# Conv block on one core: input loads ahead of the branch, tables inside the timetable, early and late steps on other engines, and a GELU output sorted by phase

## The chip, the core and the metric

The kernel runs on one core of a Trainium2 chip. A core has TensorE (PE, matrix products), VectorE (DVE), ScalarE (ACT, activation functions), GpSimd (POOL) and SyncE (SP, which here only issues transfers), and 16 DMA engines that move data between HBM and the on-chip memory SBUF. Products land in PSUM, which has eight banks. Each engine works through its own instruction list in order and waits on semaphores for the others. The metric is the device time of one execution, in microseconds (us), lower is better.

## The reference

The input x has 16 samples of 256 channels on a 64 x 64 grid, in fp32. Two residual layers follow one another. Cut to what matters:

```
x = x + L0(gn(x))      # gn: group norm, 32 groups of 8 channels
x = x + L1(gn(x))

L0: xn = rmsnorm over channels
    q, k, v = w_qkv @ xn             # 4 heads of 32
    q = softmax over head channels;  k = softmax over pixels
    context = k v^T;  out = context^T q * scale
    out = rmsnorm(w_out @ out + b_out)

L1: router: softmax of a 256 -> 4 product of the pooled input, the best 2 experts, renormalised
    expert: depthwise 3x3 conv + bias, gelu, 256 x 256 pointwise product + bias
    out = weighted sum of the two chosen experts
```

## The kernel before

A small head loads the attention weights w_qkv, multiplies them by the norm's weights and tests on DVE whether all logits are small. All engines read that flag and branch: here into `pipelined_path`; the other branch, `general_path`, is not executed.

**Order of the work.** The pipelined path writes its order out by hand. Each step is a small function with a key. A table PLAN gives each key a place in "slots"; the place of a step is the start of its phase for its sample, plus its group's offset, plus PLAN[key]. All steps are sorted by place and issued in that order, so PLAN fixes every engine's instruction list. A sample's period is 64 slots. Five phases run staggered, so that several samples are under way at once: "in" (first statistics of sample b), "q" (projections and attention context, 8 groups of 512 pixels), "out" (attention output, again 8 groups), "route" (second statistics, router, choice of experts), and "x" (the experts, 4 quarters of 16 rows). Sample 0 has nothing before it, sample 15 nothing behind it.

**The steps by line.** The rows of x that end up as output live in a ring of seven tiles; L117 loads them, for sample 0 right after the branch. For the statistics of later samples L244 loads a second copy (xa) and L247 a third (xb) for the norm, each in pieces of 512 KB (both halves of the channels), two buffers each. Statistics are L253 on DVE; L263 and L274 are small PE products of the group norm. The norm is L293 on ACT. PE transposes (L301), ACT squares and sums per token (L308), the scale r is made by L228 on DVE and L229 (a power) on POOL. With r ACT writes the scaled transposed pixels (L314, `x_keep`) and, after the projection on PE (L330), the exponentials (L338). PE adds up the context (L348); DVE and POOL normalise q (L358, L359, L363), PE turns it (L371), ACT keeps it (L374). L381 to L416 mix the context with w_out; L413 is that product, called pm. In "out" PE forms po (L424), ACT its squares (L432), DVE the scaled output ob (L443, `out_norm`), PE turns it back (L450), DVE adds it to the ring (L459), ACT squares it for the second norm (L466). The router's product pz is L509.

In "x" the experts work on two halves of the channels. The first half goes through PE: ACT pads it (L641), SP writes it to HBM and reads it back spread over partitions (`lay`, `spread`, tiles xr, 12 buffers), PE multiplies it by taps (L701), ACT applies GELU (L709). The second half goes through DVE: ACT pads it (L683) and starts the accumulator acc (L716), DVE adds eight taps for each of the two experts (L723, a 128 x 1024 operation), ACT applies GELU in place (L730). The pointwise product adds both halves up in four PSUM banks, one for each phase q (row and column odd or even): L742 multiplies acc, reading every second column of every second row, and L750 multiplies xr with 32-row tiles. DVE adds the result and the bias to the ring (L759, `residual`), SP stores it (L765). The blended expert weights come from L573 and L575 on DVE.

**Constants.** The weights for all this are loaded on ACT's queue at the start of the branch (L169 to L197), 25 transfers, and 36 small DVE operations (L209) build a table of taps from them.

Of the kernel before, what the change touches and what calls it, by code (L numbers as in the profile page):

```python
# [46 lines left out]
FC = 4 * (QA + 1) * PC  # L47
NRING = 7
# [4 lines left out]
    "load_a": -9.25, "stats": -5.66, "load_b": -8.65, "load_x1": -2.78, "mean": 2.06, "means": 2.28,  # L53
    "dev": 3.53, "devs": 8.08, "scale": 11.68, "bias": 12.33, "in_lead": 22.04, "norm0": -5.62,
    "norm1": -0.47, "turn_x0": 0.51, "x_sq0": 1.33, "x_sq1": 1.55, "turn_x1": 1.24, "x_sq2": 2.35,
    "x_sq3": 2.12, "token": 3.32, "x_keep0": 5.33, "x_keep1": 5.35, "x_keep2": 4.92,
    "x_keep3": 4.95, "project0": 4.29, "evacuate0": 5.68, "project1": 5.03, "evacuate1": 5.72,
    "project2": 5.43, "evacuate2": 6.67, "project3": 5.62, "evacuate3": 6.89, "context": 8.15,
    "q_sum": 8.09, "q_norm": 14.32, "q_turn": 15.88, "q_keep": 16.2, "mix_a": 9.74,
    "mix_turn": 9.95, "mix_v": 10.71, "mix_vv": 11.24, "mix_b": 12.36, "mix_out": 13.21,  # L60
    "mix_c": 13.7, "mix_lead": 15.67, "attend0": -0.09, "out_sq0": 0.05, "out_sq1": 0.62,
    "out_scale0": 1.38, "out_norm0": 2.98, "attend1": 0.36, "out_sq2": 1.1, "out_sq3": 1.41,
    "out_scale1": 2.74, "out_norm1": 3.53, "out_turn0": 4.46, "out_add0": 5.46, "sq_sums0": 6.37,
    "out_turn1": 5.51, "out_add1": 6.2, "sq_sums1": 7.31, "sums1": 7.7, "means1": 7.87,
    "scale1": 8.76, "router": 9.2, "route": 10.86, "choose": 12.26, "pick_taps": 15.66,
    "route_lead": 22.33, "pick_rows0": 12.84, "pick_rows1": 18.67, "pick_row_bias": 15.38,
    "weigh": 19.46, "pick_bias": 20.95, "pick000": 0.61, "pick100": 10.24, "pick001": 0.9,
    "pick101": 13.08, "pick002": 6.46, "pick102": 13.36, "pick003": 8.1, "pick103": 14.74,
    "pick010": 1.08, "pick110": 14.45, "pick011": 2.05, "pick111": 15.05, "pick012": 2.43,
    "pick112": 15.56, "pick013": 5.56, "pick113": 16.03, "lay_pw": 11.73, "spread_pw": 12.85,  # L70
    "taps0": 7.52, "taps1": 10.69, "taps2": 0.05, "taps3": -1, "taps4": 8.36, "taps5": -2.07,
    "taps6": 1.95, "taps7": 12.86, "pad1": -8.93, "start0": -2.18, "tap01": 0.61, "tap02": 0.96,
    "tap03": 1.88, "tap04": 2.18, "tap05": 2.73, "tap06": 3.26, "tap07": 5.03, "tap08": 5.6,
    "gelu10": 10.66, "start1": 4.35, "tap11": 6.15, "tap12": 6.65, "tap13": 9.14, "tap14": 9.65,
    "tap15": 11.78, "tap16": 12.21, "tap17": 13.12, "tap18": 14.18, "gelu11": 15.25, "pad00": 1.65,
    "pad01": 1.66, "lay": 4.1, "spread0": 6.9, "conv0": 10.23, "gelu00": 11.75, "spread1": 7.8,
    "conv1": 10.77, "gelu01": 12.39, "spread2": 5.25, "conv2": 10.75, "gelu02": 10.92,
    "spread3": 7.7, "conv3": 11.85, "gelu03": 12.31, "spread4": 8.85, "conv4": 12.79,
    "gelu04": 13.99, "spread5": 9.05, "conv5": 12.88, "gelu05": 14.21, "spread6": 8.74,
    "conv6": 12.33, "gelu06": 14.39, "spread7": 9.48, "conv7": 13.66, "gelu07": 14.86,  # L80
    "pw00": 16.34, "pw01": 17.04, "pw02": 18.31, "pw03": 18.34, "pw10": 19.06, "pw11": 21.05,
    "pw12": 21.16, "pw13": 21.82, "residual00": 20.82, "residual01": 23.29, "residual02": 24.4,
    "residual03": 25.27, "store0": 28.88, "residual10": 23.06, "residual11": 23.4,
    "residual12": 26.78, "residual13": 27.98, "store1": 29.6, "in_first": 5.27, "in_more": 21.33,
    "q_first": 9.02, "out_first": 11.84, "out_more": 4.06, "q_less": 0.28,
# [4 lines left out]
def pipelined_path(ctx, tc, wqkv, x, w_outT, b_out, g_out, router_wT, router_b, dw, dw_b, pwT, pw_b, out):  # L90
# [12 lines left out]
    ring = [const.tile([P, KH, 2, GT], FP, name=f"ring_{i}") for i in range(NRING)]  # L103
# [14 lines left out]

    for g in range(NG):
        load_x1(0, g)  # L120
# [48 lines left out]
    nc.scalar.dma_start(out=wout, in_=w_outT)  # L169

    bout = const.tile([P, C], FP, name="bout")
    nc.scalar.dma_start(out=bout, in_=b_out.to_broadcast([P, C]))
    nc.vector.tensor_scalar(bout, bout, 1.0 / NH, None, ALU.mult)
    gout = const.tile([P, KH], FP, name="gout")
    nc.scalar.dma_start(out=gout, in_=g_out.rearrange("(k p) -> p k", p=P))
    rw = const.tile([P, KH, NE], FP, name="rw")
    nc.scalar.dma_start(out=rw, in_=router_wT.rearrange("(k p) e -> p k e", p=P))
    nc.vector.tensor_scalar(rw, rw, 1.0 / TEMP, None, ALU.mult)
    rb = const.tile([P, NE], FP, name="rb")
    nc.scalar.dma_start(out=rb, in_=router_b.to_broadcast([P, NE]))  # L180
    nc.vector.tensor_scalar(rb, rb, 1.0 / TEMP, None, ALU.mult)
    dww = const.tile([P, NE, 10], FP, name="dww")
    nc.scalar.dma_start(out=dww[:, :, 0:9], in_=dw[P:C])
    nc.scalar.dma_start(out=dww[:, :, 9:10], in_=dw_b[P:C])
    pw = const.tile([P, KH, NE, C], FP, name="pw")
    nc.scalar.dma_start(out=pw, in_=pwT.rearrange("(k p) e o -> p k e o", p=P))
    pwb = const.tile([P, KH, NE], FP, name="pwb")
    nc.scalar.dma_start(out=pwb, in_=pw_b.rearrange("(k p) e -> p k e", p=P))

    dwc = const.tile([P, CGR, NE, 9], FP, name="dwc")
    btab = const.tile([P, CGR, NE], FP, name="btab")
    for v in range(NPC):
        vs = slice(v * CH, (v + 1) * CH)
        nc.scalar.dma_start(out=dwc[vs], in_=dw[0:P].rearrange("(g c) e t -> c g e t", c=CH))
        nc.scalar.dma_start(  # L197
            out=btab[vs], in_=dw_b[0:P].rearrange("(g c) e u -> c g (e u)", c=CH)
        )
    tab = const.tile([P, CGR, 2, 2, 2, NE], FP, name="tab")  # L200
    nc.gpsimd.memset(tab, 0.0)
    for o in range(2):
        for d in range(2):
            for p in range(2):
                for v in range(NPC):
                    ky, kx = v // 2 - o, 2 * d + 1 - v % 2 - p
                    if 0 <= ky <= 2 and 0 <= kx <= 2:
                        dst = tab[:, :, d, o, p]
                        nc.vector.scalar_tensor_tensor(  # L209
                            dst, dwc[:, :, :, 3 * ky + kx], piece[:, v : v + 1], dst,  # L210
                            ALU.mult, ALU.add,
                        )
# [30 lines left out]
    def load_a(b, g):  # L243
        nc.sync.dma_start(out=new(work, [P, KH, GT], "xa", b, g), in_=cols(x, b, g))  # L244

    def load_b(b, g):
        nc.sync.dma_start(out=new(work, [P, KH, GT], "xb", b, g), in_=cols(x, b, g))  # L247

    def stats(b, g):
        st = live["st", b] if g else new(small, [P, KH, NG, 6], "st", b, bufs=2)  # L250
        xa = live.pop(("xa", b, g)) if b else x1(b, g)
        for k in range(KH):
            nc.vector.bn_stats(st[:, k, g], xa[:, k])  # L253
# [34 lines left out]
    def norm(b, g, k):  # L288
        if k == 0:
            new(work, [P, KH, GT], "xg", b, g)  # L290
        xb = live["xb", b, g] if b else x1(b, g)
        bi, sc = live["bi", b][:, k : k + 1], live["sc", b][:, k : k + 1]
        nc.scalar.activation(live["xg", b, g][:, k], xb[:, k], AF.Identity, bias=bi, scale=sc)  # L293
# [18 lines left out]
    def x_keep(b, g, c):  # L312

        nc.scalar.activation(  # L314
            xt[g % 2][:, c, :C], live["px", b, g, c // 2][:, c % 2], AF.Copy,
            scale=live["r", b, g][:, c : c + 1],
        )
# [122 lines left out]
    def out_norm(b, g, hf):  # L440
        ob = new(work, [P, 2, C], "ob", b, g, hf, bufs=3)
        s = live.pop(("s", b, g, hf))
        nc.vector.tensor_tensor(  # L443
            ob, live.pop(("po", b, g, hf)), s.unsqueeze(2).to_broadcast([P, 2, C]), ALU.mult
        )
# [267 lines left out]
    def start1(b, j, i):  # L713
        ds = live["ds", b]
        acc = new(work, [P, QR, W], "acc", b, j, i, bufs=3)
        nc.scalar.activation(  # L716
            acc, pd1[j % 2][:, 0:QR, 0:W], AF.Identity,
            bias=ds[:, i, 9:10], scale=ds[:, i, 0:1],
        )
# [713 lines left out]
def block_kernel(ctx, tc, x, g_norm, w_qkvT, *weights_and_out):  # L1433
# [24 lines left out]
    with tc.If(small_logits > 0) as branch:  # L1458
        pipelined_path(tc, wqkv, x, *weights_and_out)
# [39 lines left out]
```

## Time and profile before

| | |
|---|---|
| median of 3 runs | 2748.02 us (2747.52 to 2748.82) |
| profiled execution | 2746.3 us |
| its span, first to last instruction | 2744.5 us |
| PE busy | 2634.1 us (96%), 19236 products |
| DVE busy | 2370.1 us (86%), 4384 instructions |
| ACT busy | 2127.0 us (78%), 5310 |
| POOL busy | 778.6 us (28%), 874 |
| bytes moved | 394.72 MB, 144 GB/s |
| transfers issued | 1024 of xr, 256 of ring, 120 each of xa and xb, 128 stores |

How to read it: "busy" counts the time in which an engine has an instruction in work. PE's instructions overlap, so the time from one start to the next says more of its rate than the length of one. One fp32 product is two passes over the array, and each pass is a row of the trace. A stage in which PE has gaps is set by something else, and a window of that stage shows which engine is full. The last sample's stage starts at about 2450 us, and the first product of the depthwise conv of sample 0 at 241.4 us.

### The profile page before, as it was taken

How to read it: one execution, taken by the hardware profiler on the slowest of the kernel's cores; microseconds unless marked ns; L12 is line 12 of the kernel's file. 1: busy time of each engine (PE TensorE's matmuls, PEld its weight loads, DVE VectorE, ACT ScalarE, POOL GpSimd, SP SyncE). 2: the span in 40 equal slices, each digit the busy share in tenths (PEclk: the TensorE clock that was granted, in tenths of full speed). 3: DMA queues.
4: the chain of work that ended last, by engine and by line, in shares of the span. 5: the costliest groups of instructions: out<-in, count | busy, mean ns of one | idle time of the engine just before them, and what ended most of it. 6: DMA issues, size and time to landing. Idle time of an engine off the chain costs nothing.

```text
span 2744.5 us, 54743 instructions
## 1 busy us (share of the span) xinstructions
PE 2634.1 (96%) x19236; PEld 2241.9 (82%) x19236; DVE 2370.1 (86%) x4384; ACT 2127.0 (78%) x5310; POOL 778.6 (28%) x874
## 2 busy tenths in 40 slices
PE   4988999999999999999999999999999999998978
PEld 3777888888888888888888888888888888886756
DVE  5459898998989899898988989899898988889996
ACT  3888878887887888888887887888788788875542
POOL 1233233233222322332232323323222233222110
PEclk9999999999999999999999999999999999999999
DMA  4335455464654545455454545546465444424332
GB/s 143 100 116 144 142 153 159 141 182 133 168 160 133 163 156 156 150 153 161 140 164 150 161 141 157 157 143 181 131 169 158 134 143 129 138 98 127 110 112 98
DMA packets 225867, 394.72 MB, mean 144 GB/s; under 512 B 22064, under 2 KB 104496, under 8 KB 225584
## 3 DMA queue, kind: packets, MB, share of 16 engines
q1 hardware_dynamic: 220704, 389.62, 46.7%
q8 instruction: 156, 2.56, 0.4%
q10 hardware_dynamic: 4880, 1.51, 0.3%
q14 instruction: 127, 1.04, 0.1%
HBM read 280.82 MB, written 110.23 MB: 142 GB/s over the span
## 4 chain that ended last, share of the span: by engine, by line
PE 85%; DVE 8%; ACT 3%; issue 2%; DMA 1%; POOL 1%; SPq 0%; ACTq 0%; POOLq 0%; DVEq 0%
PE pw L750 16%; PE pw L742 16%; PE pq L330 14%; PE dw L701 14%; PE po L424 7%; PE pc L348 7%; DVE acc L723 4%; PE tr L450 4%; PE px L301 4%; PE ptq L371 2%; DVE ring L759 1%; ACT junk L432 1%; ACT xt L314 1%; DVE ring L459 1%; ACT e L338 0%
## 5 line engine op out<-in xcount | busy, mean ns | idle before, releaser
L723 DVE SCALAR_TENSOR_TENSOR acc<-pd,ds,acc 128x1024 f32<-128x1024 f32 x1024 | 1314.2, 1286 | 5.7
L229 POOL TENSOR_TENSOR s<-s,mhalf 128x2 f32<-128x2 f32 x256 | 246.9, 966 | 1086.1 <-DVE s L228 958.6
L742 PE MATMUL pw<-acc,pw 128*128 128x256 f32 x2048 | 507.4, 392 | 22.7 <-ACT acc L730 12.5
L701 PE MATMUL dw<-xr,taps 128*128 128x256 f32 x2048 | 482.9, 380 | 8.7 <-ACT xr L709 6.0
L330 PE MATMUL pq<-wqkv_n,xg 128*128 128x256 f32 x2048 | 486.9, 382 | 2.9 <-DVE ring L459 2.9
L750 PE MATMUL pw<-xr,psp 32*128 32x256 f32 x8192 | 478.3, 381 | 0.0
L742 PEld LDWEIGHTS pw<-acc,pw 128*128 128x128 f32 x2048 | 377.9, 190 | 102.3 <-ACT acc L730 14.2
L750 PEld LDWEIGHTS pw<-xr,psp 32*128 32x128 f32 x8192 | 407.3, 185 | 63.4 <-issue 43.4
L701 PEld LDWEIGHTS dw<-xr,taps 128*128 128x128 f32 x2048 | 375.6, 190 | 59.6 <-ACT xr L709 7.7
L330 PEld LDWEIGHTS pq<-wqkv_n,xg 128*128 128x128 f32 x2048 | 374.1, 191 | 51.9 <-DVE ring L459 6.0
L759 DVE SCALAR_TENSOR_TENSOR ring<-pw,bs,ring 128x256 f32<-128x256 f32 x512 | 236.1, 474 | 97.3 <-PE pw L750 64.6
L229 POOL TENSOR_TENSOR r<-r,mhalf 128x4 f32<-128x4 f32 x128 | 185.2, 1447 | 444.7 <-DVE r L228 389.8
L308 ACT ACTIVATE jx<-px 128x256 f32<-128x256 f32 x512 | 197.5, 386 | 122.4 <-PE px L301 110.8
L466 ACT ACTIVATE sqj<-ring,nm 128x512 f32<-128x512 f32 x256 | 187.0, 730 | 123.6 <-DVE ring L459 123.4
L348 PE MATMUL pc<-xt,e 128*128 128x257 f32 x1024 | 247.3, 383 | 7.6 <-ACT e L338 7.6
L709 ACT ACTIVATE xr<-dw,bv 128x256 f32<-128x256 f32 x512 | 220.4, 478 | 43.4 <-PE dw L701 39.6
L338 ACT ACTIVATE e<-pq,r 128x256 f32<-128x256 f32 x512 | 217.6, 476 | 44.5 <-PE pq L330 43.0
L424 PE MATMUL po<-mw,qt 128*128 128x256 f32 x1024 | 249.4, 381 | 1.1 <-DVE ring L759 1.1
L459 DVE SCALAR_TENSOR_TENSOR ring<-tr,gout,ring 128x512 f32<-128x512 f32 x256 | 189.5, 747 | 63.9 <-PE tr L450 56.8
L716 ACT ACTIVATE acc<-pd,ds 128x1024 f32<-128x1024 f32 x128 | 158.5, 1238 | 110.9 <-PE pw L742 108.8
L314 ACT ACTIVATE xt<-px,r 128x256 f32<-128x256 f32 x512 | 208.7, 486 | 24.1 <-POOL r L229 22.4
L348 PEld LDWEIGHTS pc<-xt,e 128*128 128x128 f32 x1024 | 190.2, 191 | 37.7 <-ACT e L338 7.6
(138 smaller groups left out, 3487.0 us busy)
## 6 DMA issues: line engine op xcount, KB each, us to landing
xr<-lay SPq DMA_DIRECT2D x1024, 66.0 KB
ring<-in_x SPq DMA_DIRECT2D x256, 256.0 KB
out<-ring SPq DMA_DIRECT2D x128, 512.0 KB
xa<-in_x SPq DMA_DIRECT2D x120, 512.0 KB
xb<-in_x SPq DMA_DIRECT2D x120, 512.0 KB
lay<-pd SPq DMA_DIRECT2D x64, 594.0 KB
psp<-layp SPq DMA_DIRECT2D x128, 128.0 KB
layp<-pw SPq DMA_DIRECT2D x16, 256.0 KB
```

The lines of the kernel that those rows point to most:

```text
L229: nc.gpsimd.tensor_tensor(out_t, out_t, mhalf[:, :n], ALU.pow)
L314: nc.scalar.activation(xt[g % 2][:, c, :C], live["px", b, g, c // 2][:, c % 2], AF.Copy, scale=live["r", b, g][:, c : c + 1],)
L330: nc.tensor.matmul(pq, xg[:, k, c * P : (c + 1) * P], wqkv[:, k, : 2 * HID], start=(k == 0), stop=(k == KH - 1),)
L338: nc.scalar.activation(live["e", b, g][:, c], live["pq", b, g, c // 2][:, c % 2], AF.Exp, scale=live["r", b, g][:, c : c + 1],)
L348: nc.tensor.matmul(live["pc", b], live["e", b, g][:, c, HID:], xt[g % 2][:, c], start=(g == 0 and c == 0), stop=(g == NG - 1 and c == CG - 1),
L424: nc.tensor.matmul(po[:, c], qt[:, n * P : (n + 1) * P], live["mw", b], start=True, stop=True)
L701: nc.tensor.matmul(po, live[f"taps{g}", b][:, d * P : (d + 1) * P], rows3[:, :, d : d + W // 2], start=(d == 0), stop=(d == 1),)
L709: nc.scalar.activation(live["xr", b, j, g][:, 0 : GT // 2], po, AF.Gelu, bias=live["bv", b][:, g : g + 1])
L723: nc.vector.scalar_tensor_tensor(acc, pd1[j % 2][:, t // 3 : t // 3 + QR, t % 3 : t % 3 + W], live["ds", b][:, i, t : t + 1], acc, ALU.mul ...
L742: nc.tensor.matmul(po[q], live["pw1", b][:, part, ms], h[:, :, q // 2, :, q % 2], start=(part == 0), stop=False,)
L750: nc.tensor.matmul(po[q], live["psp", b][band, g, ms], live["xr", b, j, g][band, 0 : GT // 2], start=False, stop=(g == CGR - 1),)
L759: nc.vector.scalar_tensor_tensor(xo, po.rearrange("p (a c) -> p a c", c=W // 2), live["bs", b][:, m : m + 1], xo, ALU.add, ALU.add,)
```

## The change

1. The sixteen loads of x for sample 0 (256 KB each) are issued on SP before the branch; the first four ring tiles move to the head. w_qkv and its norm weights are loaded on ACT's queue.
2. The 25 weight loads become one event of the timetable (`load_weights`) on SP's queue; the scaling of three small weights and the 36 table operations become five events on DVE.
3. xa and xb are loaded in halves of 256 KB (one half of the channels each), with three half buffers for each in place of two full ones.
4. For samples 0, 1 and 2 (`b < EARLY`) `norm` and `x_keep` run on DVE instead of ACT.
5. For sample 15 `out_norm` and `residual` run on ACT instead of DVE. [...] x enters the sum in PSUM as a fifth part of the pointwise product, with the identity as weights.
6. GELU writes to a new tile h (two buffers) in which the even columns stand before the odd ones, so that the pointwise product reads 32 neighbouring columns. acc has two buffers in place of three.
7. In the last quarter of sample 15 the parts have their own places (`end_...`): first those of xr, then those of h and x, for both halves of the outputs.
8. All of PLAN has new values, and the phases of the first three and last two samples get small shifts (`x_0`, `q_1`, ...).

In general_path a pool gets smaller; it isn't executed.

```diff
+EARLY = 3
 PLAN = {
-    "load_a": -9.25, "stats": -5.66, "load_b": -8.65, "norm0": -5.62, "norm1": -0.47,
-    "gelu10": 10.66, "start1": 4.35, "gelu11": 15.25, "pw00": 16.34, "pw01": 17.04,
-    "in_first": 5.27, "in_more": 21.33, "q_first": 9.02, "out_first": 11.84, "out_more": 4.06,
...
+    "load_a0": -16.2, "load_a1": -8.65, "load_b0": -17.65, "load_b1": -7.1,
+    "stats0": -4.87, "stats1": -3.45, "norm0": -5.91, "norm1": -3.77,
+    "gelu10": 10.88, "start1": 3.82, "gelu11": 15.52, "pw00": 16.91, "pw01": 17.04,
+    "in_first": 2.74, "in_more": 1.74, "q_first": 9.11, "out_first": 7.86, "out_more": 15.48,
+    "load_weights": 21.49, "scale_weights": -2.89,
+    "spread_taps00": -8.7, "spread_taps01": -1.56, "spread_taps10": 1.5, "spread_taps11": 5.1,
+    "end_pw00": 16.45, "end_pw01": 18.13, "end_pw02": 14.45, "end_pw03": 15.46, "end_pw04": 18.16,
...
 }
...
-    for g in range(NG):
-        load_x1(0, g)
...
-    nc.scalar.dma_start(out=wout, in_=w_outT)
...
+    def load_weights():
+        nc.sync.dma_start(out=wout, in_=w_outT)
...
+        nc.sync.dma_start(out=pw, in_=pwT.rearrange("(k p) e o -> p k e o", p=P))
+    def spread_taps(o, d):
...
-    def load_a(b, g):
-        nc.sync.dma_start(out=new(work, [P, KH, GT], "xa", b, g), in_=cols(x, b, g))
+    def load_a(b, g, k):
+        nc.sync.dma_start(out=new(work, [P, GT], "xa", b, g, k, bufs=3), in_=cols(x, b, g)[:, k])
...
-        nc.scalar.activation(live["xg", b, g][:, k], xb[:, k], AF.Identity, bias=bi, scale=sc)
+        if b < EARLY:
+            nc.vector.tensor_scalar(live["xg", b, g][:, k], xb, sc, bi, ALU.mult, ALU.add)
+        else:
+            nc.scalar.activation(live["xg", b, g][:, k], xb, AF.Identity, bias=bi, scale=sc)
...
+        if b < EARLY:
+            nc.vector.tensor_scalar(dst, src, r, None, ALU.mult)
+        else:
+            nc.scalar.activation(dst, src, AF.Copy, scale=r)
...
+        if b == NB - 1:
+            for c in range(2):
+                nc.scalar.activation(ob[:, c], po[:, c], AF.Copy, scale=s[:, c : c + 1])
+        else:
+            nc.vector.tensor_tensor(ob, po, s.unsqueeze(2).to_broadcast([P, 2, C]), ALU.mult)
...
-        acc = new(work, [P, QR, W], "acc", b, j, i, bufs=3)
+        acc = new(work, [P, QR, W], "acc", b, j, i)
...
-        acc = live["acc", b, j, i]
-        nc.scalar.activation(acc, acc, AF.Gelu)
+        h = new(work, [P, 2, QR, W // 2], "h", b, j, i)
+        acc = live.pop(("acc", b, j, i)).rearrange("p r (c t) -> p t r c", t=2)
+        nc.scalar.activation(h, acc, AF.Gelu)
...
-            h = live["acc", b, j, part].rearrange("p (a o) (c t) -> p a o c t", o=2, t=2)
+            h = live["h", b, j, part].rearrange("p t (a o) c -> p t o a c", o=2)
             for q in range(4):
                 nc.tensor.matmul(
-                    po[q], live["pw1", b][:, part, ms], h[:, :, q // 2, :, q % 2],
+                    po[q], live["pw1", b][:, part, ms], h[:, q % 2, q // 2], start=begin, stop=end,
...
+        if part == 4:
+            for q in range(4):
+                nc.tensor.matmul(po[q], ident, pixels(b, j, m, q), start=begin, stop=end)
+            return
...
+        if b == NB - 1:
+            nc.scalar.activation(xo, po, AF.Identity, bias=bs)
+        else:
+            nc.vector.scalar_tensor_tensor(xo, po, bs, xo, ALU.add, ALU.add)
...
+        near = f"{b}" if b < 3 else f"e{NB - b}" if NB - b < 3 else None
+        for phase in start if near else ():
+            start[phase] += PLAN[f"{phase}_{near}"]
...
     head = ctx.enter_context(tc.tile_pool(name="head", bufs=1))
+    ring = [head.tile([P, KH, 2, GT], FP, name=f"ring_{i}") for i in range(NQ)]
+    for g in range(NG):
+        for k in range(KH):
+            nc.sync.dma_start(
+                out=ring[g // 2][:, k, g % 2],
+                in_=x[0].rearrange("(k p) t -> p k t", p=P)[:, k, g * GT : (g + 1) * GT],
+            )
...
-    nc.sync.dma_start(out=wqkv, in_=w_qkvT.rearrange("(k p) o -> p k o", p=P))
+    nc.scalar.dma_start(out=wqkv, in_=w_qkvT.rearrange("(k p) o -> p k o", p=P))
```

## The prediction

> **What bounds the kernel now.** I read the page's slices first, then windows of chosen stages, then PE's timeline. Everything below is in us of the one profiled execution.
>
> ```profile
> span 2744.5 us, 54743 instructions
> ...
> PE   4988999999999999999999999999999999998978
> ...
> DVE  5459898998989899898988989899898988889996
> ACT  3888878887887888888887887888788788875542
> ```
>
> PE is full from slice 4 to slice 35 and not full before and after. Windows show who is full instead:
>
> ```profile
> core 0: us, PE busy (x) PEld busy (x) DVE busy (x) ACT busy (x) POOL busy (x), PEclk, DMA share, GB/s
> 20.00:30.00 10.00, 0.00 (x0) 0.00 (x0) 6.01 (x13) 0.00 (x0) 0.00 (x0) 1.00 0.94 310
> 130.00:140.00 10.00, 9.29 (x52) 7.90 (x51) 4.90 (x14) 9.69 (x31) 3.16 (x5) 1.00 0.35 119
> 203.30:333.30 130.00, 122.05 (x807) 103.62 (x806) 115.91 (x216) 111.69 (x290) 42.38 (x46) 0.97 0.51 153
> 400.00:500.00 100.00, 100.00 (x701) 86.39 (x700) 88.56 (x153) 85.12 (x213) 29.79 (x29) 1.00 0.58 167
> 2449.50:2592.50 143.00, 125.54 (x1004) 101.69 (x1002) 137.14 (x239) 78.52 (x186) 33.09 (x37) 0.99 0.37 118
> 2592.50:2744.50 152.00, 122.22 (x1036) 97.23 (x1036) 125.82 (x169) 53.78 (x88) 12.33 (x19) 0.95 0.31 103
> ```
>
> At 20-30 everyone waits for x (DMA share 0.94). At 130-140 ACT is the full one with DVE half idle. The middle belongs to PE. In the last two rows DVE is the fullest (96%, 83%) and ACT half idle. A busy PE still says nothing of its rate, so I take start-to-start times from its timeline:
>
> ```profile
> 863.79 1.89 PE L330 MATMUL pq<-wqkv_n,xg 128*128 128x256 f32 x8
> 865.52 1.97 PE L742 MATMUL pw<-acc,pw 128*128 128x256 f32 x8
> 867.33 1.95 PE L330 MATMUL pq<-wqkv_n,xg 128*128 128x256 f32 x8
> ```
>
> L330 takes (865.52-863.79)/8 = 216 ns a pass, L742 (867.33-865.52)/8 = 226. In the same way L701, L424 and L348 take 216 or 217, the 128x128 transposes 109, L750 57.3. Times the counts of the page this is 2571 us of PE work, so 173 us are lost, and I place them by landmarks, each matmul's place counted off in the program's order:
>
> | stage | now | PE work | DVE work | PE after | DVE after | forecast |
> |---|---|---|---|---|---|---|
> | start to the first transpose | 36.9 | 1 | 12 | 1 | 12 | 26.5 |
> | to pm of sample 0 (L413) | 73.1 | 55 | 32 | 54 | 50 | 61.5 |
> | to its pz (L509) | 93.3 | 81 | 48 | 83 | 72 | 87 |
> | to pm of sample 2 | 129.5 | 116 | 115 | 115 | 130 | 137 |
> | to pm of sample 15 | 2116.6 | 2087 | 1894 | 2070 | 1894 | 2101 |
> | to its pz | 143.1 | 118 | 139 | 117 | 130 | 135 |
> | to the end | 152.0 | 113 | 114 | 126 | 104 | 149.5 |
>
> DVE work is counted with start-to-start times as well: a tap (L723) 1.206, L759 0.394, L443 0.60, L253 0.594, L575 0.396.
>
> **The change part by part.** *Loads ahead of the branch.* Now: loads of x are issued at 9.3, the last statistics wait ends at about 31, the first transpose comes at 36.87.
>
> ```profile
> 36.87 0.47 PE L301 MATMUL px<-ident,xg 128*128 128x128 f32 x1 [2.35 <-ACT xg L293]
> ...
> 38.27 5.55 DVE L209 SCALAR_TENSOR_TENSOR tab<-dwc,piece,tab 128x32 f32<-128x32 f32 x31
> 43.75 0.15 DVE L228 TENSOR_SCALAR r<-tss 128x4 f32<-128x4 f32 x1
> ...
> 45.02 1.57 ACT L314 ACTIVATE xt<-px,r 128x256 f32<-128x256 f32 x4 [3.81 <-POOL r L229]
> ```
>
> After: 4.2 MB of x and 0.4 MB of wqkv start at 0.8; at the 0.31 MB/us of the 20-30 row they land by about 19. wqkv now shares the engines with x, which I put at +2 for the branch (9.3 to 11.3): a load issued beside x took 4.3 (rw, issued 10.70, landed 14.95) against 2.9 alone (gn_w). DVE then needs 16 x 0.594 for statistics, 1.0 for the small tables and 0.6 for the aggregate: 22.5; the chain from there to bias is 3.4 now (32.6 to 36.0); one norm gives 26.5. Gain 10.4.
>
> *Tables as events.* L209 holds r of the first group for 5.5 us (43.75 is late by that, ACT idles 3.81). Spread over four places after group 5 they cost 36 x 0.176 = 6.3 of a DVE that is half idle. The 25 weight loads go from ACT's queue to SP's, behind three xa loads of sample 1; SP then waits for buffers anyway, and their first readers (the tables) stand some 40 us later. If that cover were gone, DVE would wait at the next xa statistics, up to 3 us. Gain with the next part.
>
> *norm and x_keep to DVE for samples 0 to 2.* A group loses 2 x 0.71 + 4 x 0.36 = 2.9 on ACT and gains 2 x 0.405 + 4 x 0.40 = 2.4 on DVE:
>
> ```profile
> L383 DVE TENSOR_SCALAR cn<-pc,rec 128x256 f32<-128x256 f32 x16 | 7.7, 484 | 0.6
> ...
> L1442 DVE TENSOR_SCALAR wqkv_n<-wqkv_n,gn_w_n 128x384 f32<-128x384 f32 x2 | 0.7, 418 | 4.2 <-DMA gn_w_n<-in_g_norm 4.2
> ```
>
> (L383 starts 0.40 apart; L573 at 256 wide 0.263, L1442 at 384 0.334, so 0.405 at 512.) The group period of sample 0 is 7.84: squares 1.9, wait for r 1.4, x_keep 1.45, exponentials 1.43, norm 0.71, q_keep 0.63, wait 0.3, all in ACT's order. After, x_keep and exponentials run side by side: 3.9 to the scale, 1.3 until DVE has the third x_keep, four contexts 1.75: 7.0, and PE alone needs 6.5. First group 7 instead of 14, seven more 7.0 to 7.2, mix 4.6: 61.5 in place of 73.1. In the next stage PE needs 9.1 a group, now 10.45 with ACT full; ACT falls from 9.7 to 6.8 and I give 9.4, plus 2: 87. Sample 2 is another matter: its groups run while sample 0 takes taps, where DVE is already full for 40 us. DVE's work there rises from 115 to 130 against 115 of PE. By DVE's order the second GELU of sample 0's first quarter is ready 53 after pz, and PE stands before its matmul at 41: 12 lost, where now it is 5. Now the stage loses 14, so 10 come on top: 115 + 12 + 10 = 137. This part costs 7 there.
>
> *GELU into a tile by phase.* L742 reads every second float of acc; L701 reads the same 8 rows of 32 floats without gaps. 226.5 against 216.2, and all 1507 ordinary passes between 400 and 2400 lie at 224 to 231, so it's not a now-and-then wait. After, h gives 32 floats in a row. The Trainium skill ("SBUF — State Buffer", the note on SBUF cachelines) speaks against a gain: two accesses to a 16-byte line give full bandwidth, so up to four fp32 of stride is free, and here the stride is two. By the rule the packing gains 0; by the row 10.3 ns x 2048 = 21, of which 1.32 a sample over the 13 of the PE-bound middle = 17 count. I take the row: same shape, only the step differs. ACT now reads with the gap; L641 does (0.62 for 256) and L293 does not (0.81 for 512, which would be about 0.60 for 256), so nothing. Two acc buffers in place of three, two of h: start of the next quarter stands 1.9 slots (4.8 us) after the GELU that frees it. One more L750 run a sample costs 0.19: 3 in all.
>
> *Half loads of xa and xb, smaller pool of the general path.* No line of the general path runs: nothing. 240 more issues at 0.37 to 0.46 on SP; spread loads queue behind them. Each half waits for its third-last to be read; in the timetable that lies 2.1 to 6.8 slots (5 to 17 us) back. Nothing, while that holds.
>
> *The last sample on ACT.* Off DVE: 16 x 0.60 (L443) and 32 x 0.394 (L759) = 22; onto ACT, half idle. Onto PE: 32 products with ident, two passes each, 226 ns: 14.5. Up to pz DVE sets the pace: 139 in 143 now, 130 at 97% = 135. After pz, the first pw waits for its weights: 46.4 of DVE work, 47.5 (now 52.7). From there PE has 92.2 of work and waits for no residual: I add 3. It ends at 142.7, not DVE. Behind it 0.8 for the residual and 6 for the store (now 2738.4 to 2744.5): 149.5. So of 22 taken off DVE 2.5 are left; PE's 14.5 takes the rest. The new order of the last quarter takes off only part of this end, in which PE works 14 after the last GELU:
>
> ```profile
> 2722.30 2.07 PE L742 MATMUL pw<-acc,pw 128*128 128x256 f32 x8 [1.55 <-ACT acc L730]
> ...
> 2731.78 3.73 PE L750 MATMUL pw<-xr,psp 32*128 32x256 f32 x64
> ...
> 2735.54 2.84 DVE L759 SCALAR_TENSOR_TENSOR ring<-pw,bs,ring 128x256 f32<-128x256 f32 x7 [6.33 <-PE pw L750]
> ```
>
> **Sum.** 26.5 + 61.5 + 87 + 137 + 2101 + 135 + 149.5 = 2697.5, against 2744.5. The profiled execution took 1.8 more than its span, and the median 1.7 more than that: 2701.
>
> **Rivals.**
> 1. *The packing pays nothing* (the 226 ns come from something else, such as four PSUM banks in turn). For: the rule; L750 too, which goes to four banks and reads without gaps, takes 229 for four. Against: L701 beside it. 2701 + 17 + 2 = 2720.
> 2. *The stages couple better than I count.* DVE's extra work for sample 2 is absorbed (the 10 on top fall away and the lateness halves: -13), and the new timetable loses 20 rather than 31 in the middle (-9): 2679. Against: 31 is what a tuned order loses now.
> 3. *Slower.* The half loads come late. Place: the SP queue, where load_b0 has 2.1 slots of lead and blocks the spread loads behind it. Price: a stall a group on PE, 13 x 8 = 104 groups. It decides from 47/104 = 0.45 us a group; at 0.6 it is 2763. For: the least margin in the new order. Against: a quarter-MB load lands 3.4 after its issue in the crowded head (9.30 to 12.74), and the shortest lead to a reader is 3.3 slots, 8.5.
> 4. *No change*: none of the savings reaches the end. Only if the head's 21 is waited off again later; PE's order has no such slack.
>
> **How the numbers follow.** Likeliest 60% (its own range 2686 to 2713, from +-6 on each of the four head and tail stages and +-5 on the middle), rival 1 22%, rival 2 13%, rival 3 3%, rival 4 2%. The range 2678 to 2724 takes in rival 1 with 4 on top and rival 2. Measurement tells 0.2% (5.5) from no change: faster 0.95, same 0.02, slower 0.03.
>
> **What would show it.** The first transpose near 26.5; group period of sample 0 near 7.0; pz of sample 0 near 175; DVE full and PE with gaps for some 60 us after it; L742's successor at 216 a pass and the sample period at 161.5 in place of 162.9; in the last 100 us PE full and DVE done about 20 before it. The forecast is wrong if the period stays 162.9 (then rival 1), if the period grows with SP waiting for xb (rival 3), or if PE has no gaps after pz (rival 2).

## The result, and the profile after

The changed kernel takes 2723.14 us (median of 4 runs, 2722.12 to 2724.97) where the kernel before, on the same chip, takes 2748.42: a ratio of 0.9906, interval 0.9889 to 0.9924. It is faster by 25, about half of the 47 that the prediction gave. The time lies inside the stated range of 2678 to 2724, but only by 1. The profiled execution took 2722.39, of which the span is 2720.7.

The page of the kernel after, its span and the slices of three engines:

```profile
span 2720.7 us, 55294 instructions
...
PE   6898999999999999999999999999999999998888
...
DVE  6889998999989898898989989898898988889984
ACT  3576788887887888788787888888788788876543
```

The first slice of TensorE shows 6 where it showed 4, since it starts 11 earlier, and VectorE ends before it, as forecast; ScalarE, which took over steps of the last sample, has more than a third of its time free there. Windows of the kernel after (columns: stretch, its length, busy time and instructions of each engine, granted clock, DMA share, GB/s):

```profile
core 0: us, PE busy (x) PEld busy (x) DVE busy (x) ACT busy (x) POOL busy (x), PEclk, DMA share, GB/s
10.00:20.00 10.00, 0.00 (x0) 0.00 (x0) 9.15 (x20) 1.28 (x1) 7.50 (x21) 1.00 0.92 298
182.20:316.90 134.70, 122.71 (x798) 103.74 (x799) 130.41 (x255) 93.24 (x246) 41.48 (x46) 0.95 0.49 148
400.00:500.00 100.00, 100.00 (x747) 86.31 (x745) 87.12 (x160) 81.68 (x202) 28.05 (x30) 1.00 0.48 157
2425.10:2563.80 138.70, 125.25 (x1007) 100.64 (x1006) 129.31 (x225) 91.42 (x219) 36.99 (x40) 1.00 0.41 125
2563.80:2720.70 156.90, 134.43 (x1100) 111.62 (x1100) 110.87 (x136) 64.09 (x119) 13.19 (x18) 0.93 0.31 100
```

In the first row VectorE takes statistics (9.15 of 10) while x still arrives; before, it was busy 6.01 of 10 in the row at 20 to 30. The last row is the surprise: after pz of sample 15 the kernel needs 156.9, and needed 152.0 before. The landmarks of the prediction's table, read in the same way:

| stage | before | forecast | after | off by |
|---|---|---|---|---|
| start to the first transpose | 36.9 | 26.5 | 26.1 | -0.4 |
| to pm of sample 0 | 73.1 | 61.5 | 71.2 | +9.7 |
| to its pz | 93.3 | 87 | 85.0 | -2.0 |
| to pm of sample 2 | 129.5 | 137 | 134.7 | -2.3 |
| to pm of sample 15 | 2116.5 | 2101 | 2108.2 | +7.2 |
| to its pz | 143.1 | 135 | 138.7 | +3.7 |
| to the end | 152.0 | 149.5 | 156.9 | +7.4 |

Three places hold the missing 23: sample 0's first stage, the steady middle, and the last sample (its last two rows). They lose 28, and the other stages win 5 of it back.

**Sample 0.** VectorE's and then TensorE's timeline of the kernel after, around the last two groups:

```profile
78.85 2.57 DVE L221 SCALAR_TENSOR_TENSOR tab<-dwc,piece,tab 128x32 f32<-128x32 f32 x9
...
82.29 2.49 DVE L221 SCALAR_TENSOR_TENSOR tab<-dwc,piece,tab 128x32 f32<-128x32 f32 x9
...
85.37 3.35 DVE L221 SCALAR_TENSOR_TENSOR tab<-dwc,piece,tab 128x32 f32<-128x32 f32 x9
88.63 0.87 DVE L331 TENSOR_SCALAR xt<-px,r 128x256 f32<-128x256 f32 x2
```
```profile
69.21 1.91 PE L364 MATMUL pc<-xt,e 128*128 128x257 f32 x8
...
78.43 1.98 PE L364 MATMUL pc<-xt,e 128*128 128x257 f32 x8 [0.22 <-ACT e L354]
...
87.02 0.66 PE L387 MATMUL ptq<-ident,e 128*128 128x128 f32 x4 [2.28 <-POOL e L379]
90.63 3.77 PE L364 MATMUL pc<-xt,e 128*128 128x257 f32 x8 [2.96 <-DVE xt L331]
```

The contexts (L364) of groups 0 to 5 follow each other at 7.35; the next two need 9.2 and 12.2. The last wait names x_keep (L331), which stands in VectorE's order behind the fourth table event (85.37). The four table events take 11 us together, not 6.3.

**The middle.** L768 of the kernel after passes at (861.84-860.11)/8 = 0.216, as forecast:

```profile
860.11 1.89 PE L768 MATMUL pw<-h,pw 128*128 128x256 f32 x8
861.84 1.04 PE L315 MATMUL px<-ident,xg 128*128 128x128 f32 x8
```

Yet the sample period is 162.20, from 162.91, not 161.5 (samples 4 to 12; so are the periods below). I took the times from each product's start to the next, less the pace of its shape, and added them up over these samples. L768 gains 1.30 a sample, of which 0.59 comes back. L779 (32-row products) stands in nine stretches a sample in place of eight; getting in and out of them and the products right behind them cost 0.42 more. Other waits cost 0.17 more.

### The profile page after: what moved, and what is told of

It is laid out like the page before. It is cut to its first block, busy times and chain, and to the rows that moved or that the text cites. A ratio compares the mean times of both kernels' runs of the same rounds, so it can differ in the third digit from the quotient of the medians.

```text
span 2720.7 us, 55294 instructions
## 1 busy us (share of the span) xinstructions
PE 2636.2 (97%) x19300; PEld 2257.1 (83%) x19300; DVE 2417.5 (89%) x4480; ACT 2083.4 (77%) x5230; POOL 767.4 (28%) x874
## 3 DMA queue, kind: packets, MB, share of 16 engines
q1 hardware_dynamic: 228880, 390.75, 46.4%
## 4 chain that ended last, share of the span: by engine, by line
PE 88%; DVE 7%; ACT 1%; issue 1%; DMA 1%; POOL 1%; SPq 0%; ACTq 0%; POOLq 0%; DVEq 0%
PE pw L779 17%; PE pw L768 16%; PE dw L719 15%; PE pq L346 14%; PE pc L364 8%; PE po L440 8%; PE px L315 4%; PE tr L468 4%; DVE acc L741 3%; PE ptq L387 2%; DMA ring<-in_x 1%; DVE ring L477 1%; DVE ring L795 1%; PE pw L774 1%; DVE st L264 0%
## 5 line engine op out<-in xcount | busy, mean ns | idle before, releaser
L242 POOL TENSOR_TENSOR s<-s,mhalf 128x2 f32<-128x2 f32 x256 | 212.2, 831 | 1103.2 <-DVE s L241 1085.4
L346 PE MATMUL pq<-wqkv_n,xg 128*128 128x256 f32 x2048 | 504.7, 384 | 0.9
L719 PE MATMUL dw<-xr,taps 128*128 128x256 f32 x2048 | 489.2, 381 | 8.4 <-ACT xr L727 6.2
L768 PE MATMUL pw<-h,pw 128*128 128x256 f32 x2048 | 480.7, 383 | 15.6 <-ACT h L750 10.0
L779 PE MATMUL pw<-xr,psp 32*128 32x256 f32 x8192 | 485.1, 382 | 0.0
L779 PEld LDWEIGHTS pw<-xr,psp 32*128 32x128 f32 x8192 | 405.9, 185 | 66.7 <-issue 47.3
L768 PEld LDWEIGHTS pw<-h,pw 128*128 128x128 f32 x2048 | 382.2, 191 | 74.3 <-ACT h L750 12.4
L795 DVE SCALAR_TENSOR_TENSOR ring<-pw,bs,ring 128x256 f32<-128x256 f32 x480 | 214.5, 475 | 66.1 <-PE pw L768 37.5
L364 PE MATMUL pc<-xt,e 128*128 128x257 f32 x1024 | 245.9, 382 | 3.6 <-DVE xt L331 3.4
L448 ACT ACTIVATE junk<-po 128x256 f32<-128x256 f32 x512 | 196.5, 384 | 25.5 <-PE po L440 20.7
L364 PEld LDWEIGHTS pc<-xt,e 128*128 128x128 f32 x1024 | 189.4, 191 | 29.0 <-issue 3.4
L440 PEld LDWEIGHTS po<-mw,qt 128*128 128x128 f32 x1024 | 190.2, 190 | 28.0 <-issue 2.0
```

Of the source, the lines that this page charges most:

```text
L242: nc.gpsimd.tensor_tensor(out_t, out_t, mhalf[:, :n], ALU.pow)
L346: nc.tensor.matmul(pq, xg[:, k, c * P : (c + 1) * P], wqkv[:, k, : 2 * HID], start=(k == 0), stop=(k == KH - 1),)
L364: nc.tensor.matmul(live["pc", b], live["e", b, g][:, c, HID:], xt[g % 2][:, c], start=(g == 0 and c == 0), stop=(g == NG - 1 and c == CG - 1),
L440: nc.tensor.matmul(po[:, c], qt[:, n * P : (n + 1) * P], live["mw", b], start=True, stop=True)
L719: nc.tensor.matmul(po, live[f"taps{g}", b][:, d * P : (d + 1) * P], rows3[:, :, d : d + W // 2], start=(d == 0), stop=(d == 1),)
L768: nc.tensor.matmul(po[q], live["pw1", b][:, part, ms], h[:, q % 2, q // 2], start=begin, stop=end,)
```

## The experiments

Times are medians; each is also given as the difference from the kernel before, measured beside it (-25.3 for the kernel after). The number in a run's name is its order. An interval is about 0.17%, 4.7 us, so small differences are read from the stages of the profiled executions. These repeat to some tenths in the middle and to 1 to 2 in sample 0's first stage and the last two.

**The tables, two edits.** First the order inside an event:

```diff
-        for p in range(2):
-            for v in range(NPC):
+        for v in range(NPC):
+            for p in range(2):
```

> The kernel after, with the two loops inside the table events swapped, so that neighbouring instructions write different slices of the table; same places, same 36 instructions. Theory (an instruction that reads what the one just before it wrote starts 0.305 us after it, an independent one 0.18): the four events take 6.7 in place of 11.0 us on VectorE, the last context of sample 0 comes about 4 earlier and the kernel takes 2719. Rival (the events are slow because of GpSimd's work beside them): still 0.305 apart, 2723. Rival (the stage is held by something else): events shorter, time 2723.

2720.70 (-28.9). In the kernel after an instruction that reads what the one before it wrote starts 0.305 later, the others 0.19. Here the dependent pairs still start 0.29 apart and the independent ones 0.17 to 0.19; nine take 1.84 to 1.94 in place of 2.5 to 2.6, the fourth event 2.65 because one instruction lasts 1.0. So the pace follows the dependence; GpSimd's work beside the events is the same in both. But pm of sample 0 moved only from 97.3 to 95.8, where 4 were expected: what holds the last group is an event's place at least as much as its length.

Then the place as well:

```diff
-            at("q", 0, NG - 1, f"spread_taps{o}{d}", spread_taps, o, d)
+            at("q", 0, 2 + 2 * o + d, "spread_taps", spread_taps, o, d)
...
-    "load_weights": 21.49,
+    "load_weights": 0, "spread_taps": 3.5,
```

> The same, and the four events stand in groups 2 to 5 of sample 0, just ahead of the scale r, where VectorE waits for the squares; the weight loads are issued ahead of the first xa loads for that. Theory (the events hold the last two groups of sample 0, 9.2 and 12.2 us in place of 7.3): all eight groups take 7.3 to 7.6, pm of sample 0 at 90 to 91 in place of 97.3, and the gain reaches the end: 2716. Rival (the time is given back in the next stage, where TensorE and VectorE are both near full): pm at 90, end at 2721 to 2723.

2717.28 (-32.3). TensorE's timeline of this kernel:

```profile
86.55 0.66 PE L387 MATMUL ptq<-ident,e 128*128 128x128 f32 x4 [0.54 <-POOL e L379]
87.52 1.98 PE L364 MATMUL pc<-xt,e 128*128 128x257 f32 x8 [0.32 <-DVE xt L331]
92.33 0.70 PE L429 MATMUL pm<-wout,ct 128*128 128x256 f32 x2
```

The waits of 2.28 and 2.96 are 0.54 and 0.32, pm stands at 92.3 in place of 97.3, and every later landmark keeps the 5: the span is 2715.7. The first of the four groups with an event still takes 7.3, the other three 7.7 to 7.8, and the last two groups 8.1 and 7.8, so that a little of the cost is left. This run has both edits; the place alone was not tried. Nothing is given back in the next stage (85.0 in both).

**The packing undone.**

```diff
-        h = new(work, [P, 2, QR, W // 2], "h", b, j, i)
-        acc = live.pop(("acc", b, j, i)).rearrange("p r (c t) -> p t r c", t=2)
-        nc.scalar.activation(h, acc, AF.Gelu)
+        acc = live["acc", b, j, i]
+        nc.scalar.activation(acc, acc, AF.Gelu)
...
-            h = live["h", b, j, part].rearrange("p t (a o) c -> p t o a c", o=2)
+            h = live["acc", b, j, part].rearrange("p (a o) (c t) -> p t o a c", o=2, t=2)
```

> The kernel after, with GELU in place again (three buffers of acc, TensorE reads every second float), timetable and all else unchanged. Theory (the packing is worth 10.3 ns a pass wherever TensorE sets the pace): L768's passes at 226.5, sample period 163.4 in place of 162.2, 2739 to 2741. Rival (the period is set by other waits and the packing is partly hidden): period 162.6, 2729 or less.

2819.02 (+69.5): both theories missed. ScalarE's start of a quarter (L734) waits for the buffer that TensorE still reads:

```profile
L734 ACT ACTIVATE acc<-pd,ds 128x1024 f32<-128x1024 f32 x128 | 159.1, 1243 | 229.9 <-PE pw L767 227.1
```

The sample period is 168.4. With three buffers the run measures the buffers, not the packing; with four, in the room of the two of acc and two of h, it measures the packing:

> As the third run, but with four buffers of acc, which take the room of the two of acc and the two of h, so that no start waits longer than in the kernel after: only what L768 reads and what GELU writes differs. Theory (10.3 ns a pass): passes at 226.5, sample period 162.2 + 1.3 = 163.5, total 2723 + 17 + 2 = 2742. Rival (the waits that the new timetable has on TensorE come out of the same slack): period 162.7, 2731. If it is as slow as the third run (2819), the third buffer was not the cause there.

2740.55 (-9.9), and its timeline:

```profile
864.76 1.97 PE L767 MATMUL pw<-acc,pw 128*128 128x256 f32 x8
866.56 1.03 PE L315 MATMUL px<-ident,xg 128*128 128x128 f32 x8
```

(866.56-864.76)/8 = 0.225, the period is 163.41, the middle 2124.0 in place of 2108.2. So the packing is worth 1.21 a sample, 15.8 in the middle and 18.3 of span. The first theory holds.

**Early samples.** `EARLY = 3` becomes 2:

> The kernel after, with norm and x_keep on VectorE for samples 0 and 1 only. Theory (VectorE is full between pz of sample 0 and pm of sample 2, and sample 2's share there costs time): that stage 128 in place of 134.7, total 2716. Rival (ScalarE is as full there, so that the work costs the same on either): stage 133 to 137, 2721 to 2726.

2719.41 (-30.2). The window between pz of sample 0 and pm of sample 2:

```profile
182.40:314.90 132.50, 122.70 (x798) 104.23 (x799) 115.51 (x215) 111.25 (x287) 44.53 (x46) 0.95 0.51 150
```

VectorE has 14.9 less to do and the stage gains 2.2 (134.7 to 132.5). The direction is the theory's, the size a third. And `EARLY = 0`:

> The kernel after with norm and x_keep on ScalarE for every sample. Theory (ScalarE is the full engine in sample 0's groups and in the stage to pz): groups of sample 0 at 7.8 in place of 7.35, stage to pm 74 to 76 in place of 71.2 (the tables still hold the last two), stage to pz 93 in place of 85, stage to pm of sample 2 at 130 to 132 in place of 134.7: total 2730 to 2733. Rival (TensorE's order holds these groups, not ScalarE): stages within 2 of those of the kernel after, 2722.

2733.51 (-16.5). The stages take 73.0, 97.2 and 131.9: against the kernel after +1.8, +12.2 and -2.8. Groups of sample 0 take 8.4 in place of 7.35, but the last two lose nearly nothing to the tables then (8.4 and 8.75), so that the first stage hardly changes. The stage to pz, of the kernel after and of this one:

```profile
97.30:182.20 84.90, 83.47 (x472) 74.08 (x472) 72.41 (x195) 63.93 (x222) 33.32 (x39) 1.00 0.39 129
```
```profile
99.40:196.60 97.20, 88.45 (x473) 73.31 (x472) 49.73 (x141) 86.59 (x276) 32.23 (x39) 1.00 0.37 113
```

ScalarE is busy 86.6 of 97.2, and with the move 63.9 of 84.9, where TensorE is full (83.5). The gain of moving norm and x_keep sits in this stage, where samples 0 and 1 both run.

**The last sample.** First the residual on VectorE again, no products with ident:

```diff
-        if b == NB - 1:
-            nc.scalar.activation(xo, po, AF.Identity, bias=bs)
-        else:
-            nc.vector.scalar_tensor_tensor(xo, po, bs, xo, ALU.add, ALU.add)
+        nc.vector.scalar_tensor_tensor(xo, po, bs, xo, ALU.add, ALU.add)
...
-        n = 5 if b == NB - 1 else 4
+        n = 4
...
-                for part in range(5 if b == NB - 1 else 4):
+                for part in range(4):
```

> The kernel after, with the residual of the last sample on VectorE again and no products with ident (32 products, 64 passes, less on TensorE); out_norm of that sample stays on ScalarE, and the last quarter keeps its new order. Theory (after the first pw of sample 15 TensorE has no gap, so its 14.5 for ident count in full, and VectorE has room for 12.6): the stretch from pz of sample 15 to the end takes 147 to 150 in place of 156.9, total 2714 to 2717. Rival (VectorE, with 12.6 more, is the bound again as it was before): 152 to 154, 2718 to 2720. Rival (residuals waiting in VectorE's order hold the taps): 157 or more, 2723 or more.

2717.28 (-33.1). Then out_norm on VectorE too:

```diff
-        if b == NB - 1:
-            for c in range(2):
-                nc.scalar.activation(ob[:, c], po[:, c], AF.Copy, scale=s[:, c : c + 1])
-        else:
-            nc.vector.tensor_tensor(ob, po, s.unsqueeze(2).to_broadcast([P, 2, C]), ALU.mult)
+        nc.vector.tensor_tensor(ob, po, s.unsqueeze(2).to_broadcast([P, 2, C]), ALU.mult)
```

> The kernel after with out_norm and the residual of the last sample both on VectorE as before; the last quarter keeps its new order. Theory (up to pz of sample 15 VectorE sets the pace, so out_norm on ScalarE is what gains there): the stage from pm to pz of sample 15 takes 144 to 147 in place of 140.4 in the sixth run, total 2721 to 2724. Rival (the new order of events gained that stage, not the engine): 139 to 141, 2717.

2722.78 (-27.2). Windows from pm to pz of sample 15 and from there to the end, of the first of these kernels and then of the second:

```profile
2427.10:2567.50 140.40, 126.92 (x1008) 101.83 (x1006) 129.37 (x225) 91.48 (x219) 37.03 (x40) 0.99 0.40 123
2567.50:2714.90 147.40, 119.75 (x1036) 98.10 (x1036) 122.90 (x168) 52.58 (x87) 13.75 (x18) 0.94 0.32 106
```
```profile
2425.10:2573.10 148.00, 131.51 (x1007) 105.90 (x1006) 139.02 (x242) 81.36 (x188) 30.61 (x40) 0.94 0.39 117
2573.10:2719.60 146.50, 120.79 (x1037) 97.75 (x1036) 122.08 (x167) 51.65 (x85) 13.29 (x18) 0.94 0.32 106
```

Together this is a ladder. All on VectorE in the new order: 148.0 + 146.5. out_norm to ScalarE: 140.4 + 147.4, a gain of 6.7. The residual too, with ident on TensorE: 138.7 + 156.9, a loss of 7.8, 9.5 of it after pz. So of the two moves one pays and one costs, and the stages of the kernel before (143.1 + 152.0) hide it, since the sums are alike. The first rung also shows what the new order does by itself, with the engines of before: 4.9 more up to pz and 5.5 less behind it.

**The old timetable in the new code.** All numbers of the timetable that both kernels have are those of before, the shifts of single samples are 0 (and pw04 18.7, so that it stays ahead of pw10):

```diff
-    "conv7": 13.97, "pw03": 18.59, "residual01": 25.47, ...
+    "conv7": 13.66, "pw03": 18.34, "residual01": 23.29, ...
```

> The kernel after with the place of every event that both kernels have put back to that of the kernel before, and the shifts of the first and last samples set to nothing; code, buffers and engines are those of the kernel after. Only the sample period in the middle is read from it. Theory (the new timetable gives back half of the packing by three waits for a PSUM bank and one run of L779 more): period 161.6, below the 162.2 of the kernel after. Rival (the smaller buffers give it back, whatever the timetable): period 162.2 to 162.9. Rival (the old timetable needs the third acc buffer): 165 and more.

2743.38 (-7.0), with a poor head (87.3 to the first pm), and a period of 161.86, the middle at 2102.9. L779 stands in eight stretches again. So the new timetable costs 0.34 a sample. Of the 1.30 gained in L768, 1.05 reach the period here. Most of the rest is one wait of 0.20 right behind a stretch of L768: TensorE's next products wait for ScalarE's x_keep, which reads a PSUM bank. That they need this bank is likely but not shown.

**What pays, together.**

> The kernel after with three edits together: the table events interleaved and placed early (second run), two early samples in place of three (fourth), the last sample's residual on VectorE without the products with ident (sixth). Theory (they sit in three stages that follow one another, and nothing is given back): the gains of 6, 3 and 7 add up, 2707 to 2710. Rival (the head's gains are waited off again): 2713 or more.

2705.38 (-44.6, ratio 0.9837, interval 0.9821 to 0.9854), faster than both kernels. Stages 26.1, 65.9, 85.2, 132.7, 2108.2, 139.0, 146.7: the edits add up. On top of it one number of the timetable:

```diff
-    "pw03": 18.59,
+    "pw03": 18.18,
```

> The eighth run's kernel with one number of the timetable changed, pw03 from 18.59 to 18.18, so that in each sample's first quarter the second half of the 32-row products (L779) follows the first at once, in place of after the four context products (L364): 8 runs of L779 a sample in place of 9. Theory (a run costs 0.09 going in and 0.25 coming out, whatever stands beside it): the sample period falls by 0.3 to 0.4 to 161.8 to 161.9, total 2700 to 2702. Rival (the switch is hidden, or the context products come late now): 2705 or more.

2703.95 (-45.4, ratio 0.984, interval 0.9827 to 0.9854), not to be told from the run before it. One stretch of L779 fewer saves 0.36 a sample, as the theory has it, but a new wait behind L768 costs 0.24 and others 0.05, and the period falls to 162.13 only. The new wait, in the weight loads of this kernel:

```profile
894.00 0.42 PEld L315 LDWEIGHTS px<-ident,xg 128*128 128x128 f32 x4 [0.46 <-DVE ob L463]
```

Moved forward by the switch saved, the second transposes of a group now come before VectorE's out_norm (L463) has read po out of its bank. The rival is right on the time, the theory on the switch.

## Why the prediction was half right

The mechanisms were mostly right. But the likeliest case (2701, its own range 2686 to 2713) missed, and the stated range held 2723 by luck: its upper end was there for rival 1, and the fifth run excludes that rival's cause. A time near a rival's number doesn't confirm the rival.

- **Loads ahead of the branch: right.** 26.1 for 26.5; the first statistics start at 11.3, as worked out.
- **Tables as events: this step failed.** "Spread over four places after group 5 they cost 36 x 0.176 = 6.3 of a DVE that is half idle." The 0.176 was read from before's stretch, where instructions of different slices stood in turn (of its first two neither waits for the other; its last three, of one slice, start 0.305 apart there too); in the new order 28 of 36 read what the one just before them wrote, and nine take 2.5 to 3.4. And "half idle" holds for groups 1 to 5; in the last two, statistics of sample 1 and its means share VectorE, and x_keep waits in the same order. Two groups lost 1.9 and 4.9 against 7.35: 6.8 of the 9.7. The second run took 5.5 of these 6.8 away; the other 1.3 stayed. The rest is the groups themselves. The first ended 8.1 after the first transpose and not 7, and the others took 7.35 for 7.0 to 7.2: TensorE's order has a group's context (1.75) ahead of the next group's transposes, and the wait for r stayed at 1.3 to 1.4.
- **norm and x_keep: mechanism right, one size off.** The stage to pz is 85.0 for 87. Sample 2's share was to cost 7 and costs 2.2. Another 2.4 of its stage is not this part's: without the move it takes 131.9, and before 129.5; what makes that stays open.
- **Packing: right**, and here rule and row decide. The Trainium skill ("SBUF — State Buffer", note on SBUF cachelines) lets a stride of two fp32 pass free; L767 in place takes 225 to 226 ns and L768 216, with the timetable, the room for buffers and all else alike. So the measurement decides. 1.21 a sample for the 1.32 forecast. The 2720 of rival 1 was close to the measured time all the same.
- **The middle: "One more L750 run a sample costs 0.19: 3 in all" was mis-sized.** It costs 0.42 with the products behind the stretches, and the new timetable adds 0.17 of other waits, for which the sum had nothing: over 13 samples 3.0 and 2.2 of the 7.2. (The sum itself is off by 1 to 2: 2116.6 - 17 + 3 is 2102.6, and its table has 2101.) A saved pass reaches the period only where no bank, buffer or order takes its place; the eleventh run saved 0.36 of switches and kept 0.07.
- **Half loads: right.** In the middle (400 to 2400) neither the statistics nor the norm wait:

```profile
L307 ACT ACTIVATE xg<-xb,bi,sc 128x512 f32<-128x512 f32 x197 | 160.5, 815 | 0.0
L264 DVE BATCH_NORM_STATS2 st<-xa 128x6 f32<-128x512 f32 x178 | 121.5, 683 | 0.0
```

- **The last sample up to pz: right on the work, not on its share.** VectorE's work is 129.3 for 130, but it fills 93% of the stage and not 97%: 138.7 for 135.
- **The last sample behind pz: this step failed.** "So of 22 taken off DVE 2.5 are left; PE's 14.5 takes the rest" was 2.5 of gain after pz; measured is 4.9 of loss. Of the 7.4 between them 5.1 lie ahead of the first pw, which came 52.6 after pz and not 47.5:

```profile
2563.80:2616.40 52.60, 38.25 (x301) 30.89 (x301) 50.37 (x88) 20.19 (x35) 10.77 (x13) 0.88 0.37 97
```

VectorE is busy 50.4 there, not 46.4, and 51.8 of 52.8 in the kernel before. It does 26 taps in both, and its residuals there belong to sample 14 and were not moved: nothing was taken off this stretch. The sixth run, with sample 15's residuals on VectorE again, has the first pw at 51.6. From the first pw to its last product TensorE needed 96.6, near the forecast (95.2). But without ident it needs only 88.5: the waits for VectorE that the products replaced were worth 6.4, and the products cost 14.5. Moving work to the engine that ends the chain was the error.

This is how the tail's end looks after; the chain that ends last runs through these products:

```profile
2709.35 1.89 PE L768 MATMUL pw<-h,pw 128*128 128x256 f32 x8
2711.07 1.97 PE L774 MATMUL pw<-ring,ident 128*128 128x256 f32 x8
```

## What to carry to other kernels

When work is moved off a full engine, count it at the price of the order it lands in: a table of dependent small instructions placed just ahead of a short wait cost more than the whole group it stood in could hide, and reordered and placed where VectorE waited anyway, it cost little. A move to another engine is a gain only in the stage where the old engine sets the pace and the new one doesn't; the same list of steps held one such move (out_norm, +6.7) and one of the other kind (residual as products, -7.8), and only taking them apart showed it. A pace read per pass held here, but in a full pipeline check what the freed time runs into next.

## What the runs showed of the hardware

- **Dependence on VectorE.** For 32 elements a partition, an instruction that reads what the one just before it wrote starts 0.29 to 0.305 us after it; an independent one 0.17 to 0.19.
- **Switching between 32-row and 128-row products.** TensorE's timeline of the eighth run, with L779 in a short and a long stretch:

```profile
885.77 1.46 PE L440 MATMUL po<-mw,qt 128*128 128x256 f32 x6
887.16 2.01 PE L779 MATMUL pw<-xr,psp 32*128 32x256 f32 x32
889.10 0.66 PE L387 MATMUL ptq<-ident,e 128*128 128x128 f32 x4
...
897.85 3.74 PE L779 MATMUL pw<-xr,psp 32*128 32x256 f32 x64
901.52 1.13 PE L346 MATMUL pq<-wqkv_n,xg 128*128 128x256 f32 x4
```

Thirty-two passes hold TensorE for 889.10-887.16 = 1.94 and 64 for 901.52-897.85 = 3.67, so cutting a stretch of 64 in two costs 0.21. The way in adds 887.16-885.77-6 x 0.216 = 0.09, and the first product behind a stretch takes 0.06 to 0.10 more than its pace: 0.36 to 0.40 for one more stretch. The Trainium skill ("TensorEngine Tiling (Array Packing)", Key Properties) says that a change of tiling mode drains the engine; the times fit that, and this is the price here.
- **The clock after an idle.** In the kernel after, TensorE waits 7.81 for GELU. That wait, and the window behind it:

```profile
2587.59 3.78 PE L768 MATMUL pw<-h,pw 128*128 128x256 f32 x8 [7.81 <-ACT h L750]
```
```profile
2587.50:2591.30 3.80, 3.71 (x8) 2.52 (x9) 3.76 (x6) 3.80 (x9) 0.00 (x0) 0.50 0.09 33
```

Eight passes take 3.7 in place of 1.8 at a granted clock of 0.50. The Trainium skill ("TensorE: Matmul & The Clock Gate", What's actually happening) gives half rate after an idle window; the row agrees. So this wait of 7.8 costs about 9.7, an estimate from these two rows.
